# Layer 1 of a four-layer state-space kernel: which engine forms delta·u·B for half of the scan units, and where their decays lie

## The chip, the cores and the metric

The kernel runs on one core of a Trainium2 chip, in one launch, in float32. The metric is the device time of that launch in microseconds; the time of a kernel is the median of several runs.

## The reference

An image batch x (4 x 64 x 64 x 192) goes through four residual layers, each of which takes x plus a mixer of the group-normalized x. Layers 0 and 3 are two-dimensional selective scans in four directions, layer 2 is a Toeplitz mixer, and layer 1, which the change concerns, is four Mamba blocks: rows forward and backward, columns forward and backward. Each line of 64 pixels is a sequence of its own. With 384 inner channels (DI) and 16 states (DS) a block computes:

```python
def mamba_block(xs, in_w, cw, cb, xw, dtw, dtb, Alog, Dv, ow):
    ...
    uc = silu(uc + cb[None, :, None])                      # causal conv over 4 taps
    x_dbl = jnp.einsum('nld,ed->nle', uc, xw)
    dt, Bp, Cp = jnp.split(x_dbl, [DT_RANK, DT_RANK + DS], axis=-1)
    delta = jax.nn.softplus(jnp.einsum('nlr,dr->nld', dt, dtw) + dtb)
    A = -jnp.exp(Alog)
    def step(h, inp):
        d_t, b_t, c_t, u_t = inp
        dA = jnp.exp(d_t[:, :, None] * A)
        h = dA * h + (d_t * u_t)[:, :, None] * b_t[:, None, :]
        y = jnp.einsum('nds,ns->nd', h, c_t)
        return (h, y)
    ...
    y = jnp.moveaxis(ys, 0, 1) + uc * Dv
    y = y * silu(z)
    return jnp.einsum('nld,cd->nlc', y, ow)
```

For every channel and state there are thus a decay `dA`, an input `delta * u * B`, the recurrence `h`, and the product of `h` with C summed over the states.

## The kernel before, in words

Layer 1 has 4 blocks x 4 images x 8 chunks = 128 jobs of 512 pixels (8 lines of 64). A job (a "chunk") covers 384 channels in 3 tiles `t` of 128, each of two halves `c` of 64 channels. The 16 states are done in 4 pairs `p`: a unit (t, p, c) holds 64 channels x 2 halves of the states on the 128 partitions, and 2 x 512 elements along the free axis. That gives 24 units a chunk. `run_jobs` walks over all units of all chunks in one sequence; the list `TWO` gives the order of the eight units of a tile.

At position i of the sequence `run_jobs` issues, in this order:

- `feed` of unit i + 2 (`AHEAD`): it makes the two operands of the scan. The input `b` of an ordinary unit is made by TensorE in PSUM, as matmuls of `dtuT` (delta·u, transposed) with diagonal matrices `diag` that hold B, and the decays `dA` are made by ScalarE as exp(A·delta) (line 347) in one of three fixed SBUF tiles. The first element of each line has decay 0. For a *direct* unit the input is a tile `bs` that `spread` made in SBUF, and the decays go into the PSUM tile `wide` (its name in the profile is `b`), after a copy of zeros into the line starts (line 335).
- `scan` of unit i: one VectorE `tensor_tensor_scan` of 128 x 1024 (line 357) gives `h` in SBUF, then GpSimd multiplies `hc = h * cbc` (line 369), where `cbc` is C broadcast over the partitions.
- `spread` of unit i + 3 (`EARLY`), if it is direct: GpSimd multiplies `bs = dtu2 * bbc` (line 301), delta·u by B, both loaded from DRAM with broadcast.
- `collect`: TensorE sums `hc` over the states into `y` with the matrix `fold` (line 387).
- steps with a fixed position: the projections, the convolution (`input_of`, VectorE line 747), the step size and softplus, transposes, gate, output, and the loads.

Direct units before are those of pair 3, both halves: 6 of the 24, all on GpSimd. The three other pairs need `diag` tiles of B, 16 ScalarE instructions a pair and chunk (line 282). `plan` gives each load (`c`, `bc`, `both`, `dtu2`, `diag`) the position at which it is issued, after the last use of the tile whose buffer it takes. The loads go through SyncE's queue. Buffers: 3 of `h`, 5 of `hc`, 2 of `wide`/`b` in PSUM, 1 of `bs`, 4 each of `c` and `diag`, 2 of `bc`.

Layers 0 and 3 use the same functions with a state carried between chunks; their direct units are on GpSimd with decays in PSUM, and their `dtu = delta * u` (line 233) is a VectorE multiply, where layer 1's is GpSimd's. The engines' streams are filled in program order per engine, with the tile framework's ordering where nothing depends.

Of the kernel before, what the change touches and what calls it, by code (L numbers as in the profile page):

```python
# [27 lines left out]

TWO = [(0, 0), (0, 1), (3, 0), (1, 1), (1, 0), (3, 1), (2, 0), (2, 1)]
ONE = [(0, 0), (3, 0), (1, 0), (2, 0)]  # L30
LAST = 2
LEAD = 12
LEAD_DIAG = 10
D1, PD, KD = 576, 96, 6
# [2 lines left out]
class Kernel:  # L37
# [66 lines left out]
    def run_jobs(self, jobs, pools):  # L104


        G = jobs[0]["DI"] // 64
        order = []
        for t in range(-(-G // 2)):
            order += [(t, *one) for one in (TWO if 2 * t + 1 < G else ONE)]  # L110
        units = [(k, *one) for k in range(len(jobs)) for one in order]
        per = len(order)
        steps = {}
        for k, job in enumerate(jobs):
            for at, step in self.prepare(job, pools) + job["steps"]:
                steps.setdefault(k * per + at, []).append(step)
        for at, load in self.plan(jobs, order, pools):
            steps.setdefault(at, []).append(load)
        start, end = min(steps), max(len(units) + 3, max(steps) + 1)
        waiting = []  # L120
        for i in range(min(start, -EARLY), end):
            if 0 <= i + AHEAD < len(units):
                k, t, p, c = units[i + AHEAD]
                self.feed(jobs[k], t, p, c, pools)
            todo = waiting[:1]
            if 0 <= i < len(units):
                k, t, p, c = units[i]
                self.scan(jobs[k], t, p, c, pools)
            if 0 <= i + EARLY < len(units):
                k, t, p, c = units[i + EARLY]  # L130
                if c in jobs[k]["direct"].get(p, ()):
                    self.spread(jobs[k], t, p, c, pools)
            if 0 <= i < len(units):
                if (i + 1) % 2 == 0:
                    waiting += [(units[i][0], [one[1:] for one in units[i - 1 : i + 1]], n) for n in range(2)]


            if todo:
                k, two, n = waiting.pop(0)
                self.collect(jobs[k], two, n, pools)  # L140
                if n and two[1][1] == LAST:
                    jobs[k]["add"](two[0][0])
            for step in steps.get(i, []):
                step()

    def plan(self, jobs, order, pools):
# [3 lines left out]
        for k, job in enumerate(jobs):  # L150
            job["cbc"], job["bbc"], job["diag"], job["both"], job["dtu2"] = {}, {}, {}, {}, {}
            when = {name: k * len(order) + at for name, at in job["when"].items() if isinstance(at, int)}

            near = 2 if job["carry"] is not None else 5
            dtu = when["finish"] + 3 if job["carry"] is not None else when["store"] + 5
            for j, (t, p, c) in enumerate(order):
                i, g = k * len(order) + j, 2 * t + c
                direct = c in job["direct"].get(p, ())
                reads = [("c", p, i, when["project"] + 5), ("both", g, i - AHEAD, when["finish"] + near)]
                if direct:  # L160
                    reads += [("bc", p, i - EARLY, when["project"] + 5), ("dtu2", g, i - EARLY, dtu)]
                else:
                    reads.append(("diag", p, i - AHEAD, when["turn_b"] + 5))
                for name, key, at, after in reads:
                    first, _ = uses.setdefault(name, {}).get((k, key), (at, at))
                    uses[name][k, key] = first, at
                    ready[name, k] = after
        loads = []
        for name, of in uses.items():
            bufs, turn = pools["bufs"][name], sorted(of, key=of.get)  # L170
            for j, (k, key) in enumerate(turn):
                first = of[k, key][0]
                at = max(ready[name, k], first - LEAD)
                if j >= bufs:
                    at = max(at, of[turn[j - bufs]][1] + pools["behind"])
                one = lambda part=None, job=jobs[k], name=name, key=key: self.fetch(job, name, key, pools, part)
                if name == "diag":

                    at = max(ready[name, k], first - LEAD_DIAG)
                    if j >= bufs:  # L180
                        at = max(at, of[turn[j - bufs]][1] + 3)
                    loads += [(first, at + part, lambda part=part, one=one: one(part)) for part in range(NB)]
                    at += NB - 1
                else:
                    loads.append((first, at, one))
                assert at < first, (name, k, key, at, first)
# [104 lines left out]
    def spread(self, job, t, p, c, pools):  # L291

        g = 2 * t + c
        b = pools["work"].tile([128, 2 * T], F32, name="bs", bufs=1)
        if job["carry"] is None:
            by = lambda one: one.rearrange("p (h n l) -> p h n l", h=2, n=2)
            dtu = job["dtu2"][g].rearrange("p (h l) -> p h l", h=2).unsqueeze(2).broadcast_to([128, 2, 2, 256])
        else:
            by = lambda one: one.rearrange("p (n l) -> p n l", n=2)
            dtu = job["dtu2"][g].unsqueeze(1).broadcast_to([128, 2, T])  # L300
        self.nc.gpsimd.tensor_mul(by(b), dtu, by(job["bbc"][p]))  # L301
        job["bs"][t, p, c] = b

    def feed(self, job, t, p, c, pools):
# [1 line left out]
        nc = self.nc  # L306
        w, rev, g = job["w"], job["rev"], 2 * t + c
        lines = job["carry"] is None
        direct = c in job["direct"].get(p, ())
        wide = pools["b"].tile([128, 2 * T], F32, name="b")  # L310
        if direct:
            b = job["bs"].pop((t, p, c))
        else:
# [15 lines left out]
        if lines:  # L329
            if job.get("begin"):  # L330
                job.pop("begin")()
            if direct:
                dA = wide
                at = HW - 1 if rev else 0
                nc.scalar.copy(dA[:, at::HW], job["zero"])  # L335
            else:
                self.turns_dA += 1
                dA = job["dA"][self.turns_dA % len(job["dA"])]
            inner = slice(0, HW - 1) if rev else slice(1, HW)
            of = delta.rearrange("p (h a b) -> p h a b", h=2, b=HW)[:, :, :, inner]  # L340
            to = dA.rearrange("p (h n a b) -> p h n a b", h=2, n=2, b=HW)[:, :, :, :, inner]
# [27 lines left out]
        nc.gpsimd.tensor_mul(hc, h, job["cbc"][p])  # L369
        job["done"][t, p, c] = hc  # L370

    def collect(self, job, units, n, pools):

        nc = self.nc
        t, first, _ = units[0]
        last = units[1][1]
        units = sorted(units, key=lambda one: one[2])
        if first == 0 and n == 0:
            job["y"][t] = pools["y"].tile([128, T], F32, name="y")
        y = job["y"][t]  # L380
        for c, unit in enumerate(units):
# [3 lines left out]
            else:  # L385
                of = one[:, n * T : (n + 1) * T]
            nc.tensor.matmul(  # L387
                y[c * 64 : (c + 1) * 64, :], self.fold, of, start=first == 0 and n == 0, stop=last == LAST and n == 1
            )

    def neg_exp(self, A):
# [97 lines left out]
    def ss2d_scan(self, pre, u_d, y_d, P, NT, ways, A, dtb):  # L489
# [3 lines left out]
        with (  # L493
# [17 lines left out]
                for g in range(DI // 64) for p in range(PAIRS)  # L511
            }
            when = {
                3: dict(load=-33, project=-29, turn_b=-27, step_size=(-21, -19, -17), finish=-15,
                        turn=(-13, -11, -9), direct={3: (1,)}),
                2: dict(load=-25, project=-21, turn_b=-19, step_size=(-17, -16), finish=-14,
                        turn=(-9, -8), direct={3: (0, 1)}),
            }[NT]
            direct = when["direct"]

            for k, (col, rev) in sorted(enumerate(ways), key=lambda one: one[1]):
# [7 lines left out]
                for c in range(NCH - 1, -1, -1) if rev else range(NCH):  # L529
# [28 lines left out]
                    if rev:  # L558
# [1 line left out]
                            steps.append((8 * t + 2, lambda t=t, earlier=earlier: earlier(t)))  # L560
                    job.update(
                        P=P, NT=NT, DI=DI, k=k, w=w, rev=rev, carry=carry, first=first, add=add, y={}, fed={},
                        done={}, bs={}, when=when, steps=steps, direct=direct,
                    )
                    jobs.append(job)
            self.run_jobs(jobs, pools)
# [64 lines left out]
    def mamba(self, x_in):  # L631
# [6 lines left out]
        done = [self.image_tiles(f"m_out{i}_") for i in range(2)]  # L638

        both_w = [self.dram.tile([P, NT, C], F32, name=f"m_both_w{i}") for i in range(4)]  # L640
        bufs = dict(c=4, bc=2, diag=4, both=4, dtu2=2)
        with (
            tc.tile_pool(name="n", bufs=2) as pn,
            tc.tile_pool(name="n_ps", bufs=2, space=PSUM) as psum,
# [27 lines left out]
        with (  # L672
# [14 lines left out]
            pools = {"prep": prep, "work": work, "c": cp, "diag": dp, "both": both, "mm": mm, "b": bp, "y": yp,  # L687
                     "bc": bcp, "dtu2": dtu2, "bufs": bufs, "behind": 2}
            fixed = [once.tile([P, 2 * T], F32, name=f"dA{j}") for j in range(3)]
            zero = once.tile([P, 2 * ROWS], F32, name="zero")  # L690
            nc.gpsimd.memset(zero, 0.0)
            jobs = []
            for i in range(4):
                rev, w = i % 2 == 1, {}
                xs = by_row if i < 2 else by_col
                for b in range(B):
                    for c in range(NCH):
                        begin = b == 0 and c == 0
                        jobs.append(self.mamba_job(
                            pw, pin, mm, i, begin, rev, w, xs[b], done[i // 2][b], both_w[i], c, fixed, zero  # L700
                        ))
            self.run_jobs(jobs, pools)
        return list(zip(*done))

    def mamba_job(self, pw, pin, mm, i, begin, rev, w, x, done, both_w, c, fixed, zero):

        nc, ins = self.nc, self.i
        P, NT = 128, 3
# [72 lines left out]
                nc.scalar.copy(o, ps)  # L781
            nc.sync.dma_start(done[:, m, s], o)

        when = dict(project=-24, turn_b=-22, step_size=(-20, -18, -17), finish=-15, turn=(-10, -7, -3), store=-11)
        each = lambda f, ats: [(at, lambda t=t: f(t)) for t, at in enumerate(ats)]
        steps = [(-50, weights)] if begin else []
        steps += [(-48, load)] + each(input_of, (-45, -32, -29)) + each(gate, (-6, -4, -2)) + each(out, (32, 35))
        if rev:
            steps += each(earlier, (26, 29))
        job.update(  # L790
            P=P, NT=NT, DI=DI, w=w, rev=rev, carry=None, first=True, dA=fixed, y={}, fed={}, done={}, bs={},
            add=gated, when=when, steps=steps, begin=start_lines if begin else None, direct={3: (0, 1)},
            zero=zero,
        )
        return job

# [309 lines left out]
```

## Time and profile before

| what | value |
|---|---|
| median of 3 runs | 31,847.99 us (31,831.84 to 31,864.97) |
| the profiled execution's own time | 31,794.9 us |
| its span | 31,793.1 us, mean granted TensorE clock 0.948 |
| layer 1's scans, first to last | 11,042.1 to 22,312.9 us |
| busy share of the whole span | PE 89%, DVE 71%, ACT 73%, POOL 71% |
| busy share, 12,000 to 22,000 us | PE 95%, DVE 72%, ACT 82%, POOL 88% |

PE is TensorE, DVE is VectorE, ACT is ScalarE, POOL is GpSimd, and SP is SyncE. A line of the profile names the source line, the engine, the operation, the tiles as output<-inputs, shapes, and the count, then the busy time in us and the mean duration of one in ns, and after the second bar the time the engine stood idle before these instructions with what ended it. Matmuls overlap, so a count times a mean can exceed the busy time; a float32 matmul appears as two instructions. In the timeline a line has the start in us and the duration in us first; neighbours of one kind are merged (x2, x3).

### The profile page before, as it was taken

Reading aid. Unit: us, or ns where it says so; the run is one execution under the profiler, and the core shown is the slowest. Engines: PE = TensorE matmul, PEld = TensorE weight load, DVE = VectorE, ACT = ScalarE, POOL = GpSimd, SP = SyncE. Lnnn points to the kernel's source line nnn. Section 1 sums busy time; section 2 is a strip of 40 time slices with the busy share of each in tenths; the row PEclk is TensorE's granted clock in tenths of the full one; section 3 lists DMA queues with packets and bytes.
Section 4 is the critical chain, followed back from the end, with each engine's and each line's share of the span. In section 5 each row is a group of like instructions: output and inputs, shape, how many; then the busy total and the mean of one; then the engine's idle time right before and its main releaser. Section 6 shows DMA issues by size and latency. Waiting matters only on the chain. (4 is left out here: it accounts for less than half of the span.)

```text
span 31793.1 us, 449637 instructions
## 1 busy us (share of the span) xinstructions
PE 28311.3 (89%) x162840; PEld 13772.2 (43%) x162840; DVE 22474.8 (71%) x16587; ACT 23362.1 (73%) x50239; POOL 22678.0 (71%) x9755
## 2 busy tenths in 40 slices
PE   8997998999899699999999999999588988888888
PEld 4453554454445344444444444444355343434344
DVE  7887887788788677777777777777433267676767
ACT  7885885887688488888888888888133287878788
POOL 6884885888488488888888888888000086767777
PEclk9998999999999899999999999999788999999999
DMA  3333333333333423233333333333533444444444
GB/s 101 100 97 110 99 97 107 103 98 98 109 100 97 135 93 93 93 97 98 98 98 96 95 95 95 98 98 99 132 72 72 109 129 120 128 124 125 124 124 124
DMA packets 1565670, 3326.87 MB, mean 105 GB/s; under 512 B 343781, under 2 KB 356438, under 8 KB 1546934
## 3 DMA queue, kind: packets, MB, share of 16 engines
q1 hardware_dynamic: 1403702, 3021.19, 34.7%
q10 hardware_dynamic: 159744, 276.91, 2.6%
q8 instruction: 1289, 21.12, 0.3%
q14 instruction: 935, 7.66, 0.1%
HBM read 2137.94 MB, written 656.08 MB: 88 GB/s over the span
## 5 line engine op out<-in xcount | busy, mean ns | idle before, releaser
L369 POOL TENSOR_TENSOR hc<-h,c 128x1024 f32<-128x1024 f32 x7680 | 18189.2, 2384 | 3115.9 <-DVE h L364 1317.7
L324 PE MATMUL b<-diag,dtuT 128*64 128x256 f32 x98304 | 12805.9, 391 | 800.1 <-DVE h L364 679.9
L324 PEld LDWEIGHTS b<-diag,dtuT 128*64 128x64 f32 x98304 | 7507.3, 140 | 6835.9 <-issue 3091.1
L387 PE MATMUL y<-hc,fold 128*64 128x512 f32 x30720 | 8995.0, 598 | 587.4 <-POOL hc L369 572.6
L364 DVE TENSOR_TENSOR_SCAN h<-dA,carry,b 128x512 f32<-128x512 f32 x6720 | 8195.0, 1264 | 1805.9 <-PE b L324 1134.3
L347 ACT ACTIVATE dA<-both,A 128x512 f32<-128x512 f32 (+1 forms) x12288 | 8279.8, 711 | 203.0 <-DVE h L357 182.0
L357 DVE TENSOR_TENSOR_SCAN h<-dA,b 128x1024 f32<-128x1024 f32 x2304 | 5251.7, 2284 | 2047.7 <-PE b L324 883.2
L282 ACT ACTIVATE diag<-ident,bt 128x128 f32<-128x128 f32 x20480 | 6527.3, 391 | 124.5 <-ACT b L347 86.1
L301 POOL TENSOR_TENSOR bs<-dtu,bc 128x1024 f32<-128x1024 f32 x1536 | 3638.4, 2369 | 1479.7 <-DMA c<-bc_dram 1087.9
L387 PEld LDWEIGHTS y<-hc,fold 128*64 128x64 f32 x30720 | 2497.6, 138 | 2981.7 <-POOL hc L369 1262.0
L441 POOL MEMSET pad<- 128x13068 f32 (+1 forms) x8 | 73.4, 9177 | 3977.5 <-DMA inw<-in_L_in_w 3004.7
L347 ACT ACTIVATE b<-both,A 128x504 f32<-128x504 f32 (+1 forms) x3072 | 2078.1, 676 | 412.7 <-DVE h L364 379.8
L357 DVE TENSOR_TENSOR_SCAN h<-b,bs 128x1024 f32<-128x1024 f32 x768 | 1754.1, 2284 | 659.6 <-ACT b L347 391.2
L367 ACT COPY carry<-h 128x2 f32<-128x2 f32 x4608 | 851.4, 185 | 1367.1 <-DVE h L364 1165.5
L364 DVE TENSOR_TENSOR_SCAN h<-b,carry,bs 128x512 f32<-128x512 f32 x1344 | 1638.0, 1259 | 105.7 <-POOL hc L369 95.3
L364 DVE TENSOR_TENSOR_SCAN h<-dA,b 128x512 f32<-128x512 f32 x960 | 1112.9, 1205 | 436.2 <-ACT dA L347 175.8
L347 ACT ACT_TABLE_LOAD x1018 | 1306.1, 1283 | 15.0 <-ACT b L335 0.3
L730 PE MATMUL in_ps<-xn,in_w 96*128 96x512 f32 x1536 | 933.4, 738 | 329.4 <-DMA xn<-m_row 177.8
L747 DVE SCALAR_TENSOR_TENSOR u<-in_ps,conv_w,u 128x504 f32<-128x504 f32 (+2 forms) x1152 | 835.7, 725 | 460.3 <-ACT u L742 438.6
L233 DVE TENSOR_TENSOR dtu<-delta,u 128x1536 f32<-128x1536 f32 (+1 forms) x256 | 611.4, 2388 | 758.2 <-ACT delta L232 602.9
L242 PEld LDWEIGHTS dtu_ps<-ident,dtu 128*128 128x128 f32 (+1 forms) x4096 | 422.1, 142 | 875.7 <-issue 569.3
L730 PE MATMUL z_ps<-xn,in_w 96*128 96x512 f32 x1536 | 761.7, 618 | 0.0
(155 smaller groups left out, 22077.8 us busy)
## 6 DMA issues: line engine op xcount, KB each, us to landing
c<-bc_dram SPq DMA_DIRECT2D x3072, 256.0 KB
both<-delta SPq DMA_DIRECT2D x2048, 128.0 KB
bc<-bc_dram SPq DMA_DIRECT2D x768, 256.0 KB
both<-delta_dram SPq DMA_DIRECT2D x768, 256.0 KB
dtu<-dtu_dram SPq DMA_DIRECT2D x768, 256.0 KB
dtu<-dtu SPq DMA_DIRECT2D x1280, 128.0 KB
L_y<-out ACTq DMA_DIRECT2D x512, 256.0 KB
u<-L_u SPq DMA_DIRECT2D x160, 768.0 KB
```

The source lines that it names most:

```text
L233: (nc.gpsimd if job["carry"] is None else nc.vector).tensor_mul(job["dtu"], delta, job["u"])
L282: nc.scalar.activation(to, self.ident, AF.Copy, scale=of)
L301: self.nc.gpsimd.tensor_mul(by(b), dtu, by(job["bbc"][p]))
L324: nc.tensor.matmul(to, job["dtuT"][:, k, g * 64 : (g + 1) * 64], job["diag"][p][:, k, 2 * q : 2 * q + 2, :], start=True, stop=True,)
L347: nc.scalar.activation(to[n], of, AF.Exp, scale=w["A"][:, g, 2 * p + n : 2 * p + n + 1])
L357: nc.vector.tensor_tensor_scan(h[:, way], dA[:, way], b[:, way], 0.0, ALU.mult, ALU.add)
L364: nc.vector.tensor_tensor_scan(hn[:, n, way], dA[:, n, way], by_n[:, n, way], start, ALU.mult, ALU.add)
L367: nc.scalar.copy(carry[g, p], hn[:, :, 0 if rev else T - 1])
L369: nc.gpsimd.tensor_mul(hc, h, job["cbc"][p])
L387: nc.tensor.matmul(y[c * 64 : (c + 1) * 64, :], self.fold, of, start=first == 0 and n == 0, stop=last == LAST and n == 1)
L730: nc.tensor.matmul(ps, w["in_w"][:, k, to + t * P : to + (t + 1) * P], job["xn"][:, k, :], start=k == 0, stop=k == KC - 1,)
L747: nc.vector.scalar_tensor_tensor(u[:, :, to], ps[:, :, of], tap(3 - j), u[:, :, to], ALU.mult, ALU.add)
```

## The change

In layer 1 direct units become those of pairs 1 and 3: 12 of the 24 units of a chunk. For (1, 0), (1, 1) and (3, 0) `spread` runs on VectorE, for (3, 1) on GpSimd: with three tiles, nine and three a chunk. `direct` is now a dictionary from (pair, half) to engine. A direct unit of layer 1 takes its decays from the same three fixed SBUF tiles `dA` as the others and no PSUM tile, and the copy of zeros is gone. The order of units in a tile becomes `LINES`, in which ordinary and direct units alternate; `collect` learns from `run_jobs` which pair of units is the first and last of a tile (`ends`). There are two `bs` buffers in layer 1, three of `bc` and three of `diag`; a `diag` buffer is refilled 2 positions after its last use in layer 1 in place of 3; some steps move by one to six positions. Layers 0 and 3 keep their units, engines and order.

```diff
+LINES = [(0, 0), (3, 1), (2, 0), (1, 1), (0, 1), (3, 0), (2, 1), (1, 0)]
...
-                if c in jobs[k]["direct"].get(p, ()):
+                if (p, c) in jobs[k]["direct"]:
                     self.spread(jobs[k], t, p, c, pools)
...
-                        at = max(at, of[turn[j - bufs]][1] + 3)
+                        at = max(at, of[turn[j - bufs]][1] + pools["behind"])
...
     def spread(self, job, t, p, c, pools):
-        b = pools["work"].tile([128, 2 * T], F32, name="bs", bufs=1)
+        b = pools["work"].tile([128, 2 * T], F32, name="bs", bufs=2 if job["carry"] is None else 1)
...
-        self.nc.gpsimd.tensor_mul(by(b), dtu, by(job["bbc"][p]))
+        job["direct"][p, c].tensor_mul(by(b), dtu, by(job["bbc"][p]))
...
     def feed(self, job, t, p, c, pools):
-        direct = c in job["direct"].get(p, ())
-        wide = pools["b"].tile([128, 2 * T], F32, name="b")
+        direct = (p, c) in job["direct"]
+        wide = None if direct and lines else pools["b"].tile([128, 2 * T], F32, name="b")
...
-            if direct:
-                dA = wide
-                at = HW - 1 if rev else 0
-                nc.scalar.copy(dA[:, at::HW], job["zero"])
-            else:
-                self.turns_dA += 1
-                dA = job["dA"][self.turns_dA % len(job["dA"])]
+            self.turns_dA += 1
+            dA = job["dA"][self.turns_dA % len(job["dA"])]
...
     def mamba(self, x_in):
-        bufs = dict(c=4, bc=2, diag=4, both=4, dtu2=2)
+        bufs = dict(c=4, bc=3, diag=3, both=4, dtu2=2)
...
-        when = dict(project=-24, turn_b=-22, step_size=(-20, -18, -17), finish=-15, turn=(-10, -7, -3), store=-11)
+        when = dict(project=-23, turn_b=-21, step_size=(-19, -18, -17), finish=-15, turn=(-9, -7, 3), store=-11)
...
-        steps += [(-48, load)] + each(input_of, (-45, -32, -29)) + each(gate, (-6, -4, -2)) + each(out, (32, 35))
+        steps += [(-48, load)] + each(input_of, (-45, -33, -29)) + each(gate, (-5, -3, -1)) + each(out, (33, 35))
...
-            add=gated, when=when, steps=steps, begin=start_lines if begin else None, direct={3: (0, 1)},
-            zero=zero,
+            add=gated, when=when, steps=steps, begin=start_lines if begin else None, turns=LINES,
+            direct={(1, 0): nc.vector, (1, 1): nc.vector, (3, 0): nc.vector, (3, 1): nc.gpsimd},
```

More of the change, by code (lines that the diff above doesn't have):

```diff
@@ L30 @@
 ONE = [(0, 0), (3, 0), (1, 0), (2, 0)]
-LAST = 2
+LINES = [(0, 0), (3, 1), (2, 0), (1, 1), (0, 1), (3, 0), (2, 1), (1, 0)]
 LEAD = 12
@@ L109, in run_jobs @@
         for t in range(-(-G // 2)):
-            order += [(t, *one) for one in (TWO if 2 * t + 1 < G else ONE)]
+            order += [(t, *one) for one in (jobs[0]["turns"] if 2 * t + 1 < G else ONE)]
         units = [(k, *one) for k in range(len(jobs)) for one in order]
@@ L134, in run_jobs @@
                 if (i + 1) % 2 == 0:
-                    waiting += [(units[i][0], [one[1:] for one in units[i - 1 : i + 1]], n) for n in range(2)]
+                    tile = units[i][:2]
+                    ends = [j < 0 or j >= len(units) or units[j][:2] != tile for j in (i - 2, i + 1)]
+                    waiting += [(units[i][0], [one[1:] for one in units[i - 1 : i + 1]], n, ends) for n in range(2)]
             if todo:
-                k, two, n = waiting.pop(0)
-                self.collect(jobs[k], two, n, pools)
-                if n and two[1][1] == LAST:
+                k, two, n, ends = waiting.pop(0)
+                self.collect(jobs[k], two, n, ends, pools)
+                if n and ends[1]:
                     jobs[k]["add"](two[0][0])
@@ L308, in feed @@
         lines = job["carry"] is None
-        direct = c in job["direct"].get(p, ())
-        wide = pools["b"].tile([128, 2 * T], F32, name="b")
+        direct = (p, c) in job["direct"]
+        wide = None if direct and lines else pools["b"].tile([128, 2 * T], F32, name="b")
         if direct:
@@ L370, in scan, with collect @@
         job["done"][t, p, c] = hc
-    def collect(self, job, units, n, pools):
+    def collect(self, job, units, n, ends, pools):
         nc = self.nc
-        t, first, _ = units[0]
-        last = units[1][1]
+        t, (first, last) = units[0][0], ends
         units = sorted(units, key=lambda one: one[2])
-        if first == 0 and n == 0:
+        if first and n == 0:
             job["y"][t] = pools["y"].tile([128, T], F32, name="y")
@@ L387, in collect @@
             nc.tensor.matmul(
-                y[c * 64 : (c + 1) * 64, :], self.fold, of, start=first == 0 and n == 0, stop=last == LAST and n == 1
+                y[c * 64 : (c + 1) * 64, :], self.fold, of, start=first and n == 0, stop=last and n == 1
             )
@@ L514, in ss2d_scan @@
                 3: dict(load=-33, project=-29, turn_b=-27, step_size=(-21, -19, -17), finish=-15,
-                        turn=(-13, -11, -9), direct={3: (1,)}),
+                        turn=(-13, -11, -9), direct={(3, 1): nc.gpsimd}),
                 2: dict(load=-25, project=-21, turn_b=-19, step_size=(-17, -16), finish=-14,
-                        turn=(-9, -8), direct={3: (0, 1)}),
+                        turn=(-9, -8), direct={(3, 0): nc.gpsimd, (3, 1): nc.gpsimd}),
             }[NT]
@@ L562, in ss2d_scan @@
                         P=P, NT=NT, DI=DI, k=k, w=w, rev=rev, carry=carry, first=first, add=add, y={}, fed={},
-                        done={}, bs={}, when=when, steps=steps, direct=direct,
+                        done={}, bs={}, when=when, steps=steps, direct=direct, turns=TWO,
                     )
@@ L689, in mamba @@
             fixed = [once.tile([P, 2 * T], F32, name=f"dA{j}") for j in range(3)]
-            zero = once.tile([P, 2 * ROWS], F32, name="zero")
-            nc.gpsimd.memset(zero, 0.0)
             jobs = []
@@ L699, in mamba @@
                         jobs.append(self.mamba_job(
-                            pw, pin, mm, i, begin, rev, w, xs[b], done[i // 2][b], both_w[i], c, fixed, zero
+                            pw, pin, mm, i, begin, rev, w, xs[b], done[i // 2][b], both_w[i], c, fixed
                         ))
@@ L703, in mamba, with mamba_job @@
         return list(zip(*done))
-    def mamba_job(self, pw, pin, mm, i, begin, rev, w, x, done, both_w, c, fixed, zero):
+    def mamba_job(self, pw, pin, mm, i, begin, rev, w, x, done, both_w, c, fixed):
         nc, ins = self.nc, self.i
```

## The prediction

> **What bounds layer 1 now.** I read first the busy time of each engine in a steady stretch of layer 1 (12,000 to 22,000 us), then the groups of instructions there, then single stretches of the timeline in which VectorE and GpSimd meet.
>
> The stretch, busy us by engine (PE, PEld, DVE, ACT, POOL), clock and DMA:
>
> ```profile
> 12000.00:22000.00 10000.00, 9466.04 (x50885) 4135.91 (x50882) 7181.93 (x4210) 8205.20 (x15114) 8768.51 (x3872) 0.97 0.31 97
> ```
>
> Its groups (busy us, mean ns | idle before):
>
> ```profile
> L369 POOL TENSOR_TENSOR hc<-h,c 128x1024 f32<-128x1024 f32 x2727 | 6411.3, 2368 | 1231.5 <-DVE h L357 1113.7 <-PE b L324 89.7 <-DMA c<-bc_dram 17.0
> L357 DVE TENSOR_TENSOR_SCAN h<-dA,b 128x1024 f32<-128x1024 f32 x2045 | 4661.7, 2284 | 1787.9 <-PE b L324 755.6 <-ACT dA L347 704.8 <-POOL hc L369 203.3
> L324 PE MATMUL b<-diag,dtuT 128*64 128x256 f32 x32704 | 4094.3, 392 | 102.2 <-DVE h L357 102.2
> ...
> L282 ACT ACTIVATE diag<-ident,bt 128x128 f32<-128x128 f32 x5460 | 1746.4, 390 | 91.0 <-ACT b L347 78.5 <-DMA dtu<-dtu_dram 12.5
> L301 POOL TENSOR_TENSOR bs<-dtu,bc 128x1024 f32<-128x1024 f32 x682 | 1617.7, 2372 | 0.0
> L357 DVE TENSOR_TENSOR_SCAN h<-b,bs 128x1024 f32<-128x1024 f32 x681 | 1555.3, 2284 | 578.9 <-ACT b L347 348.7 <-POOL bs L301 174.8 <-POOL dtu L233 48.9
> ```
>
> Six bs a chunk, so 682 of them are 113.67 chunks: 87.97 us a chunk, 3.67 us for each of its 24 units. Per chunk PE is busy 83.3 us (95%), POOL 77.1, ACT 72.2, DVE 63.2. PE is the fullest, and scans wait for b from it. The reader is to see one thing more: a scan takes the same 2284 ns in both forms, and hc keeps 2368 ns beside them. In both forms one of the scan's two inputs is in PSUM: b where dA is in SBUF, and the decays (tile "b") where bs is in SBUF.
>
> What a DVE instruction with two SBUF inputs does beside GpSimd is shown only in the other layers, by `dtu = delta * u` (L233). Alone, a multiply of that size takes 1758 ns; L233 takes 3030 (groups of the whole run):
>
> ```profile
> L233 DVE TENSOR_TENSOR dtu<-delta,u 128x1536 f32<-128x1536 f32 x128 | 387.9, 3030 | 442.3 <-ACT delta L232 287.0 <-DMA c<-bc_dram 155.3
> ...
> L619 DVE TENSOR_TENSOR yc<-yc,z 128x1536 f32<-128x1536 f32 x32 | 56.3, 1758 | 39.5 <-ACT yc L616 38.7
> ```
>
> The timeline (start us, duration us) in layer 0, and in layer 3 where GpSimd came second:
>
> ```profile
> 2278.42 2.37 POOL L369 TENSOR_TENSOR hc<-h,c 128x1024 f32<-128x1024 f32 x1 [1.07 <-PE b L324]
> 2279.33 3.07 DVE L233 TENSOR_TENSOR dtu<-delta,u 128x1536 f32<-128x1536 f32 x1 [1.08 <-ACT delta L232]
> ```
>
> ```profile
> 26120.84 5.66 POOL L369 TENSOR_TENSOR hc<-h,c 128x1024 f32<-128x1024 f32 x2
> ...
> 26122.05 2.23 DVE L233 TENSOR_TENSOR dtu<-delta,u 96x1024 f32<-96x1024 f32 x1
> ```
>
> Layer 0: hc ends at 2280.79, DVE at 2282.40, 1.61 us later: 1536 elements at the rate of the lone multiply, so DVE did nothing while hc ran. Layer 3: the second hc of the two ends at 26126.50, 2.22 us after DVE's end at 26124.28: it did nothing while DVE ran. DVE there ends 1.08 us after the hc it waited for (single records). The two engines exclude each other.
>
> **What the Trainium skill says.** Its page "SBUF — State Buffer", section "Who interferes with whom", says that a DVE instruction with two SBUF inputs contends with a GpSimd instruction that reads SBUF, that the one which comes second is blocked until the first is over, and that one SBUF input outside the two-port modes does not contend. The lines above agree for multiplies (both directions) and for scans with one SBUF input. No run here shows a scan with two. "VectorE: DVE Perf Modes", section "The perf-mode tier table", has float32 tensor_tensor at 1x only: agreed, L619 is 1.14 ns an element.
>
> **The change part by part, per chunk of layer 1.** The order of instructions after the change gives the counts; the other layers keep theirs.
>
> - PE: six more direct units, so 18 b units become 12. b is 4094.3/113.67 = 36.0 us, 2.0 a unit: −12.0, PE 71.
> - ACT: diagonals for two pairs in place of three: −16 x 0.32 (1746.4/5460) = −5.1; six zero copies of 172 ns: −1.0; two table loads of 1283 ns fewer: −2.6; the 12 decays move to SBUF (707 ns for 671): about 0. ACT 63.5.
> - POOL: three bs of 2.37 fewer: −7.1, POOL 70.0.
> - DVE: nine multiplies of 128x1024. Nearest row: the lone 96x1024 multiplies, 1.20 us. +10.8, DVE 74.0.
> - SP: two bc loads of 256 KB more, 0.46 us each to issue, DMA at 31%: hidden. The new turn order leaves three units between the last use of a c tile and the next chunk's first, where the tightest pair had four: at the new pace (below) 13.4 us instead of 14.7, and hc waited only 17.0 us for c in the whole stretch: 0, at worst 1 to 3 us for each of four c loads. PSUM and dA buffers: the b tiles now serve half the units, so PE's waits for a scan shrink; three diag buffers in place of four delay ACT, which has slack.
>
> By these sums alone no engine would exceed 74 us. But the 12 direct scans now read dA **and** bs from SBUF, and the nine DVE multiplies read two SBUF tensors. All 21 must exclude every GpSimd instruction, and all of GpSimd's work here reads SBUF. The added wait is on both engines: behind a blocked multiply stands the next scan on DVE, behind a blocked hc the next hc and the bs, and y on PE waits for hc.
>
> The excluded time per chunk, by durations after a handover: a direct scan 2.28 − 0.13 = 2.15 (0.13 is what the multiply's lone 1.20–1.22 exceeds its 1.08 by; applied to the scan, an estimate), a DVE multiply 1.08, hc 2.22 after DVE and 2.32 after another POOL instruction (pitch of successive hc in the stretch). DVE's order is direct scan, multiply, other scan; two units thus cost 2.15 + 1.08 + 2.22 + 2.32 = 7.77 us, while the other scan (2.28) runs beside hc. Twelve such: 93.2. Three of the multiplies are POOL's: +3 x (2.32 − 1.08) = 3.7. z in gated 3 x 1.25 = 3.8; dtu 3.4. Sum **104.2 us**, above every engine's own load, and above 87.97. DVE's convolution and gate (9.4 us, one input in PSUM) hide under hc. Idle of the shared interface: none at best, and 5.3% if it idles like PE now; I take the middle, 2.65%: 107.0 us a chunk, 4.46 a unit.
>
> 107.0 − 87.97 = 19.1 us; x128 chunks = 2,440 us. The profiled execution took 31,794.9 (span 31,793.1), so 34,235; the median of the runs is 53 above that execution: **34,290 us**. Unknown costs of this case: idle 0 gives +2,080 (33,920), idle 8% with late c loads +3,300 (35,150).
>
> **The rivals.**
>
> 1. Faster: the scan, at 2.2 ns an element half the multiply's pace, does not take the shared interface; only the nine multiplies do. Against it: the skill's rule names any two-input instruction. For it: no scan with two SBUF inputs has been seen. Then POOL decides: 70.0 + 9 x (1.08 + 2.22 − 2.32 = 0.98) = 78.8, and with PE's 5.3% idle 83.2 us: −4.8 x 128 = −610, **31,240 us**. It tips to slower if exclusion from scans exceeds 4.8/12 = 0.4 us each.
> 2. Half exclusion: the scan holds the interface for half of its time: 104.2 − 12 x 1.08 = 91.2, /0.9735 = 93.7: +730, **32,580 us**. Against it: in the multiplies the exclusion was whole.
> 3. Exclusion plus lost cover: the scheduled order leaves hc with nothing ready while other scans run, a tenth of the time: 104.2/0.89 = 117: +3,720, **35,570 us**. For it: hc waits 1113.7 us for scans already. Against it: h and hc have 3 and 5 buffers, so GpSimd can lag and keep work ready.
> 4. No effect: exclusion from scans happens to cancel PE's relief; a narrow point between 1 and 2.
>
> **How the numbers follow.** Full exclusion 0.79, rival 1 0.09, rival 2 0.07, rival 3 0.04, rival 4 0.01. A measurement of this kernel tells about 0.2% from no change. Faster 0.09, within 0.01, slower 0.90. The range leaves out rival 1 and most of 2 and 3: 32,900 to 35,300.
>
> **What would show it.** Right: in layer 1 the busy shares of PE and ACT fall to about 66% and 59% (71 and 63.5 of 107 us), while those of DVE and POOL stay high, because a blocked instruction's record is stretched by its wait (L233 above); direct scans with dA and bs have a mean well above 2284 ns, or hc well above 2368, and the multiplies well above 1200; where the two engines meet, hc ends about 2.2 us after a direct scan's end; diag falls to 32 a chunk. Wrong: direct scans and hc overlap with both at their old durations, and the chunk is about 83 us.

## The result, and the profile after

The changed kernel took 35,047.84 us (median of 4 runs, 35,042.67 to 35,054.36), the kernel before 31,839.92 us in the same comparison: a ratio of 1.1009, 95% interval 1.099 to 1.1028. It is 3,208 us slower. The forecast was 34,290 us, range 32,900 to 35,300; its mechanism is borne out by what follows, one term of its sum is not. The loss is in layer 1: its scans now run from 11,051 to 25,556 us of the profiled execution (own time 35,042.67 us), 14,504 us in place of 11,271.

The busy time of each engine in a steady stretch of layer 1 of the changed kernel, columns as before:

```profile
13000.00:24000.00 11000.00, 8356.57 (x34060) 3161.98 (x34058) 9230.93 (x4454) 6783.02 (x10943) 9708.15 (x3010) 0.89 0.26 79
```

The groups of that stretch (busy us, mean ns | idle before):

```profile
L366 POOL TENSOR_TENSOR hc<-h,c 128x1024 f32<-128x1024 f32 x2323 | 7564.1, 3276 | 918.6 <-DVE h L354 885.7 <-DMA c<-bc_dram 7.0 <-PE y L383 1.7
L354 DVE TENSOR_TENSOR_SCAN h<-dA,bs 128x1024 f32<-128x1024 f32 x1161 | 3627.7, 3125 | 703.1 <-ACT dA L344 358.2 <-POOL hc L366 329.7 <-POOL dA L754 10.1
...
L326 PE MATMUL b<-diag,dtuT 128*64 128x256 f32 x18578 | 2830.6, 400 | 154.4 <-DVE h L354 154.2
L354 DVE TENSOR_TENSOR_SCAN h<-dA,b 128x1024 f32<-128x1024 f32 x1161 | 2637.3, 2272 | 530.0 <-PE b L326 510.7 <-POOL dA L754 19.3
L303 DVE TENSOR_TENSOR bs<-dtu,bc 128x1024 f32<-128x1024 f32 x871 | 2302.6, 2644 | 21.6
...
L303 POOL TENSOR_TENSOR bs<-dtu,bc 128x1024 f32<-128x1024 f32 x290 | 1065.8, 3675 | 0.0
L284 ACT ACTIVATE diag<-ident,bt 128x128 f32<-128x128 f32 x3104 | 980.8, 388 | 0.0
```

2323 hc are 96.8 chunks: **113.7 us a chunk**, where before it was 88.0. Diagonals are 32 a chunk, as the diff says. The scans with one SBUF input (dA and b) kept their time, 2272 ns. Everything that reads two SBUF tensors grew: the direct scans to 3125 ns, the VectorE multiplies to 2644 (1.2 alone), hc from 2368 to 3276, GpSimd's bs from 2372 to 3675. These records hold waiting time, as the timeline of the changed kernel shows (start us, duration us; each line a neighbour of the one before on the other engine):

```profile
18029.37 4.64 POOL L366 TENSOR_TENSOR hc<-h,c 128x1024 f32<-128x1024 f32 x2
18031.75 4.42 DVE L354 TENSOR_TENSOR_SCAN h<-dA,bs 128x1024 f32<-128x1024 f32 x1 [3.40 <-POOL hc L366]
18033.97 4.34 POOL L303 TENSOR_TENSOR bs<-dtu,bc 128x1024 f32<-128x1024 f32 x1
18036.20 3.19 DVE L303 TENSOR_TENSOR bs<-dtu,bc 128x1024 f32<-128x1024 f32 x1
```

The two hc end at 18034.01. The direct scan, on record since 18031.75, ends 2.16 us later, at 18036.17. The bs of GpSimd, on record since 18033.97, ends 2.14 us after the scan, and the VectorE multiply 1.08 us after that. The four run one after the other though their records overlap by half: **the scan with two SBUF inputs excludes GpSimd just as the multiply does.**

To measure this over the whole stretch I put GpSimd's instructions and VectorE's two-input ones in the order of their ends, and count for each the time from the later of its own start and the end before it. Where an instruction was already waiting at that end, the means are 2.155 us for a direct scan (the prediction's 2.15), 1.083 for a VectorE multiply (1.08), 2.18 for hc behind VectorE (2.22) and 2.31 behind GpSimd (2.32). Per chunk all these records cover 103.3 us, where the prediction's sum was 104.2. For 10.4 us none of them is on record; that I call the idle time of the interface, which stands for whatever it is that the two engines cannot use at once. The same count for the kernel before gives 77.2 covered and 10.8 idle.

### The profile page after: what moved, and what is told of

Same layout as the page of the kernel before. It is cut to its first block, busy times and chain, and to the rows that moved or that the text cites. A ratio compares the mean times of both kernels' runs of the same rounds, so it can differ in the third digit from the quotient of the medians.

```text
span 35040.9 us, 424437 instructions
## 1 busy us (share of the span) xinstructions
PE 28695.3 (82%) x150552; PEld 13290.8 (38%) x150552; DVE 26610.9 (76%) x17739; ACT 23085.3 (66%) x47679; POOL 25626.4 (73%) x9370
## 5 line engine op out<-in xcount | busy, mean ns | idle before, releaser
L366 POOL TENSOR_TENSOR hc<-h,c 128x1024 f32<-128x1024 f32 x7680 | 20946.8, 2744 | 2927.7 <-DVE h L361 1381.5
L383 PE MATMUL y<-hc,fold 128*64 128x512 f32 x30720 | 10270.2, 654 | 3548.5 <-POOL hc L366 3548.5
L326 PE MATMUL b<-diag,dtuT 128*64 128x256 f32 x86016 | 11929.6, 394 | 883.4 <-DVE h L361 680.4
L344 ACT ACTIVATE dA<-both,A 128x512 f32<-128x512 f32 (+1 forms) x13824 | 9175.7, 710 | 2411.3 <-DVE h L354 2313.9
L284 ACT ACTIVATE diag<-ident,bt 128x128 f32<-128x128 f32 x18432 | 5855.7, 390 | 26.4 <-issue 0.9
L354 DVE TENSOR_TENSOR_SCAN h<-dA,bs 128x1024 f32<-128x1024 f32 x1536 | 4815.9, 3135 | 922.9 <-ACT dA L344 469.2
L354 DVE TENSOR_TENSOR_SCAN h<-dA,b 128x1024 f32<-128x1024 f32 x1536 | 3489.0, 2271 | 679.1 <-PE b L326 658.0
L303 DVE TENSOR_TENSOR bs<-dtu,bc 128x1024 f32<-128x1024 f32 x1152 | 3040.9, 2640 | 37.6 <-DMA dtu<-dtu_dram 9.1
L361 DVE TENSOR_TENSOR_SCAN h<-b,carry,bs 128x512 f32<-128x512 f32 x1344 | 1638.3, 1260 | 104.2 <-POOL hc L366 93.6
L344 ACT ACT_TABLE_LOAD x1146 | 1470.3, 1283 | 20.2 <-DMA both<-delta_dram 3.0
L344 ACT ACTIVATE b<-both,A 128x512 f32<-128x512 f32 x1536 | 1047.1, 682 | 409.5 <-DVE h L361 378.9
L759 POOL TENSOR_TENSOR z<-z,u 128x512 f32<-128x512 f32 x384 | 752.6, 1960 | 487.3 <-DVE u L758 477.3
L744 ACT ACT_TABLE_LOAD x381 | 488.8, 1283 | 787.9 <-DVE u L741 785.6
```

What stands on the lines that cost most here:

```text
L284: nc.scalar.activation(to, self.ident, AF.Copy, scale=of)
L303: job["direct"][p, c].tensor_mul(by(b), dtu, by(job["bbc"][p]))
L326: nc.tensor.matmul(to, job["dtuT"][:, k, g * 64 : (g + 1) * 64], job["diag"][p][:, k, 2 * q : 2 * q + 2, :], start=True, stop=True,)
L344: nc.scalar.activation(to[n], of, AF.Exp, scale=w["A"][:, g, 2 * p + n : 2 * p + n + 1])
L354: nc.vector.tensor_tensor_scan(h[:, way], dA[:, way], b[:, way], 0.0, ALU.mult, ALU.add)
L361: nc.vector.tensor_tensor_scan(hn[:, n, way], dA[:, n, way], by_n[:, n, way], start, ALU.mult, ALU.add)
```

## The experiments

All are timed against the kernel before on the same chip, whose median was 31,832 to 31,846 us in these comparisons; the changed kernel's own time is the one above. The idle and the covered time are counted as above, between 13,000 and 21,500 us.

**One part alone: decays in SBUF.** The kernel before, whose six direct units stay on GpSimd, with their decays in the fixed SBUF tiles:

```diff
-        wide = pools["b"].tile([128, 2 * T], F32, name="b")
+        wide = None if direct and lines else pools["b"].tile([128, 2 * T], F32, name="b")
...
-            if direct:
-                dA = wide
-                at = HW - 1 if rev else 0
-                nc.scalar.copy(dA[:, at::HW], job["zero"])
-            else:
-                self.turns_dA += 1
-                dA = job["dA"][self.turns_dA % len(job["dA"])]
+            self.turns_dA += 1
+            dA = job["dA"][self.turns_dA % len(job["dA"])]
```

> The kernel before with one part of the change alone: its six direct units a chunk (all on GpSimd) take their decays from the fixed SBUF tiles, without zero copies. Theory (exclusion): the six direct scans have a mean well above 2284 ns where they come second; the excluded time is 77.2 + 6 x 2.15 - 6 x 0.14 = 89.3 us a chunk, with 2 to 11 us of idle 91.5 to 100 us, so 32,300 to 33,400 us. Rival (a scan does not need the shared interface, the multiplies on VectorE made the loss): no slower than before, 31,500 to 31,900 us, since PSUM is relieved.

32,538.16 us, ratio 1.022 (1.0205 to 1.0235). The groups of this kernel in the stretch:

```profile
L352 DVE TENSOR_TENSOR_SCAN h<-dA,b 128x1024 f32<-128x1024 f32 x1631 | 3715.3, 2283 | 1676.6 <-ACT dA L342 671.9 <-POOL hc L364 443.6 <-PE b L324 264.0
L352 DVE TENSOR_TENSOR_SCAN h<-dA,bs 128x1024 f32<-128x1024 f32 x544 | 1831.5, 3367 | 71.1 <-POOL bs L301 59.2 <-ACT dA L342 0.5
```

```profile
L364 POOL TENSOR_TENSOR hc<-h,c 128x1024 f32<-128x1024 f32 x2175 | 5985.2, 2776 | 454.5 <-DVE h L352 450.4 <-issue 2.0 <-PE in_ps L725 1.5
```

No multiply has moved, yet scans with two SBUF inputs take 3367 ns and those with one 2283, and hc is 408 ns longer than before. Covered time 89.0 us a chunk (expected 89.3), idle 4.8, chunk 93.8. The exclusion by scans is shown by itself: moving one operand from PSUM to SBUF costs about 700 us with six such scans a chunk. The edit also makes the three fixed decay tiles serve all 24 units in place of 18; but the covered time alone, 89.0 us, is already more than the 88.0 us of a whole chunk before, and VectorE's waits for decays hold 1.0 us of the idle here against 1.4 before, so late decays do not make the loss.

**Another part alone: multiplies on VectorE.** The kernel before with its six multiplies on the other engine:

```diff
-        self.nc.gpsimd.tensor_mul(by(b), dtu, by(job["bbc"][p]))
+        (self.nc.vector if job["carry"] is None else self.nc.gpsimd).tensor_mul(by(b), dtu, by(job["bbc"][p]))
```

> The kernel before with another part alone: its six multiplies for bs a chunk on VectorE in place of GpSimd, decays in PSUM. Theory (exclusion whole but short for multiplies): excluded time 77.2 - 6 x 2.32 + 6 x 1.08 = 69.8 us, VectorE 63.2 + 6 x 1.2 and up to 1.2 us of waiting for each, 78 us at most, PE unchanged at 83 of 88 us: within 1% of before, 31,550 to 32,150 us. Rival (VectorE multiplies stall the scans in front of GpSimd so that most of the loss comes from them): above 32,500 us.

31,868.73 us, ratio 1.0012 (1.0003 to 1.0021). The VectorE multiplies of this kernel:

```profile
L301 DVE TENSOR_TENSOR bs<-dtu,bc 128x1024 f32<-128x1024 f32 x576 | 1172.4, 2035 | 11.2
```

Each waits 0.8 us on average (2035 − 1.2 us alone), and still the covered time falls to 69.8 us a chunk, as expected, and the time stays; the idle is 18.7 us, and TensorE, 92% busy, is the fullest engine here too. The multiplies exclude GpSimd too, but briefly, and they free more of GpSimd (2.32 us each) than they take (1.08). By themselves they are not the loss.

**The change with its decays back in PSUM.** `dA = wide` with its PSUM tile and the zero copy as in the lines removed above, all else as changed.

> The changed kernel with the decays of its 12 direct units a chunk back in PSUM (and the zero copies back); the nine VectorE and three GpSimd multiplies, the unit order and the step positions stay as changed. Theory (scans with two SBUF inputs exclude GpSimd): every scan is back at about 2284 ns and hc beside a scan at 2368; the excluded time falls from the 103.3 us a chunk measured after the change by 12 x 2.16 to about 77 us; with 2 to 10 us of idle a chunk that is 79 to 87.5 us, so 30,750 to 31,850 us in all. Rival (the VectorE multiplies, the unit order or the smaller diag and larger bc pools cost the time): it stays above 33,500 us.

33,048.72 us, ratio 1.038 (1.0363 to 1.0398): 2,000 us faster than the changed kernel, but above what the theory allowed. The groups of this kernel in the stretch:

```profile
L373 POOL TENSOR_TENSOR hc<-h,c 128x1024 f32<-128x1024 f32 x2084 | 5546.1, 2679 | 1203.8 <-DVE h L361 1086.9 <-DMA c<-bc_dram 92.3 <-PE y L390 1.1
...
L361 DVE TENSOR_TENSOR_SCAN h<-b,bs 128x1024 f32<-128x1024 f32 x1041 | 2372.6, 2279 | 462.3 <-ACT b L351 462.0 <-issue 0.3
L361 DVE TENSOR_TENSOR_SCAN h<-dA,b 128x1024 f32<-128x1024 f32 x1042 | 2369.9, 2274 | 495.1 <-PE b L328 375.4 <-ACT dA L351 82.9 <-POOL hc L373 23.2
```

Both kinds of scan are back at 2.28 us, and the covered time falls from 103.3 to 79.4 us. But the idle rises from 10.4 to 18.5: the interface no longer decides, and scans wait for decays and for b in PSUM, and the gate for y. So about 2,000 of the 3,208 us go with the exclusion by scans. The order, the pools and steps of the change, or twelve direct units on two PSUM tiles, carry a cost of their own of about 1,200 us when that exclusion is gone; which of them it is, no run separates.

**Where the idle of the changed kernel comes from.** The idle was the term furthest from the forecast, so five runs went to it. The largest waits of VectorE between 13,000 and 24,000 us (96.8 chunks; total us, times, longest us):

```profile
DVE h L354 <- PE b L326: 510.7, 97, 5.6
DVE u L758 <- PE y L383: 507.4, 97, 6.0
DVE h L354 <- ACT dA L344: 358.2, 94, 4.2
DVE h L354 <- POOL hc L366: 329.7, 97, 3.4
```

A wait of VectorE leaves the interface idle only if GpSimd has nothing to do meanwhile. Laid over the idle time (13,000 to 21,500 us), the wait for b holds 3.1 us of it a chunk and the gate's wait for y 3.0; the waits for decays and for hc hold none, since GpSimd works through them. Another 3.5 us pass while an ordinary scan runs and GpSimd has no new h. The place of the gate in the timeline:

```profile
18074.64 3.32 POOL L366 TENSOR_TENSOR hc<-h,c 128x1024 f32<-128x1024 f32 x1 [2.29 <-DVE h L354]
18078.01 3.59 PE L383 MATMUL y<-hc,fold 128*64 128x512 f32 x8 [2.94 <-POOL hc L366]
...
18081.68 0.75 DVE L758 SCALAR_TENSOR_TENSOR u<-u,D,y 128x512 f32<-128x512 f32 x1 [5.93 <-PE y L383]
...
18082.44 2.28 DVE L354 TENSOR_TENSOR_SCAN h<-dA,b 128x1024 f32<-128x1024 f32 x1
18082.51 1.27 POOL L759 TENSOR_TENSOR z<-z,u 128x512 f32<-128x512 f32 x1 [4.55 <-DVE u L758]
```

hc ends at 18077.96, y needs it, the gate (L758) needs y, and the next scan stands behind the gate in VectorE's queue; GpSimd, with no new h, waits 4.55 us. The place of b comes next:

```profile
18092.37 1.98 PE L383 MATMUL y<-hc,fold 128*64 128x512 f32 x4 [1.73 <-POOL hc L366]
...
18094.13 1.07 PE L326 MATMUL b<-diag,dtuT 128*64 128x256 f32 x4
...
18095.38 2.29 DVE L354 TENSOR_TENSOR_SCAN h<-dA,b 128x1024 f32<-128x1024 f32 x1 [5.26 <-PE b L326]
```

In TensorE's queue y, which waits for hc, stands in front of b.

First, the convolution's nine VectorE instructions a chunk left out, taps and all:

```diff
-            for j in range(1, 4):
+            for j in range(4, 4):
                 to, of = slice(j, HW), slice(0, HW - j)
```

> The changed kernel without the nine VectorE instructions a chunk of layer 1's convolution (the taps other than the last are left out of the computation, 6.5 us of VectorE a chunk). In the changed kernel the shared interface stands idle 10.4 us a chunk, 5.3 of them in one place: ScalarE waits for the convolution on VectorE, the decays behind it come late, and the direct scan with them. Theory: that idle goes, and the chunk falls by 4 to 6 us to 108 to 110 us, 34,300 to 34,550 us in all. Rival (the convolution was hidden under hc, as predicted, and the idle has another cause): within 0.5% of the changed kernel, 34,900 to 35,200 us.

34,967.39 us, ratio 1.0983 (1.0966 to 1.0999); idle 10.3, as in the changed kernel; the 80 us are little more than the noise of the two ratios. The theory missed because it had laid 5.3 us of the idle to late decays; in the trace of the changed kernel they stand at the scan that waits for b, 3.1 us of waiting and 2.2 us in which that scan itself runs. VectorE's wait for decays did fall, from 277.9 to 88.3 us in the stretch, but no idle was behind it. The wait for b stayed, behind the same y:

```profile
17034.81 7.47 POOL L366 TENSOR_TENSOR hc<-h,c 128x1024 f32<-128x1024 f32 x2 [0.98 <-DVE h L354]
...
17042.34 1.97 PE L383 MATMUL y<-hc,fold 128*64 128x512 f32 x4 [1.73 <-POOL hc L366]
17044.10 1.07 PE L326 MATMUL b<-diag,dtuT 128*64 128x256 f32 x4
...
17045.34 2.29 DVE L354 TENSOR_TENSOR_SCAN h<-dA,b 128x1024 f32<-128x1024 f32 x1 [5.26 <-PE b L326]
```

The second hc ends at 17042.28, y follows at once, then b, then the scan. Second, therefore, `collect` (y, and with it the gate) one unit later in layer 1:

```diff
...
-            todo = waiting[:1]
+            todo = waiting[(1 if jobs[0]["carry"] is None and i < len(units) else 0) :][:1]
```

> The changed kernel with the summing matmuls (y from hc, in collect) and the gate that follows them one unit later in layer 1. In the changed kernel the shared interface stands idle 10.4 us a chunk. Theory: the idle comes from in-order queues behind hc: y waits for a late hc at the head of TensorE's queue with the b matmuls of coming scans behind it, and the gate on VectorE waits for y with the next scan behind it. Then the idle falls to 3 to 6 us a chunk, 34,050 to 34,500 us in all. Rival (idle from late decays or from too few tiles in flight): within 0.5% of the changed kernel, or slower because the five hc buffers are held longer, 34,900 us or more.

34,691.31 us, ratio 1.0898 (1.0882 to 1.0914): 357 us faster than the changed kernel, idle 7.5 us. The direction is the theory's, the size about half of the middle of what it expected: the idle in the waits for b and y falls from 6.1 to 0.9 us, but that beside ordinary scans rises from 3.5 to 5.1, and 1.0 us in waits for decays is new. Third, both edits:

> The changed kernel with collect one unit later in layer 1 and also without the nine VectorE instructions a chunk of the convolution (the taps other than the last are left out of the computation). Idle of the shared interface so far, us a chunk: changed kernel 10.4, without convolution 10.3, collect later 7.5, where the largest idle left (3.0) stands at a direct scan whose decays come late from ScalarE, which waited for the convolution. Theory: the two causes mask each other, so with both gone the idle falls to 2 to 5 us and the chunk to 105 to 108 us, 33,950 to 34,350 us in all. Rival (what is left has a third cause): idle stays at 7 us or more, 34,600 us or more.

34,504.8 us, ratio 1.0838 (1.0822 to 1.0854), idle 6.3. Between theory and rival: the convolution is worth 187 us here and about 80 alone, so its cost is in part masked, but 6 us stay. Some of VectorE's waits left in this kernel:

```profile
DVE u L758 <- PE y L383: 536.7, 110, 7.0
DVE h L354 <- ACT dA L344: 221.2, 77, 5.6
DVE h L354 <- PE b L326: 140.7, 78, 1.8
```

The idle of these kernels, us a chunk from 13,000 to 21,500 us, by what VectorE does meanwhile (small remainders left out; in the kernel before it is GpSimd's idle time; 10.3 is the 10.4 above, in the shorter stretch):

| kernel | scan waits for b | gate waits for y | scan waits for decays | an ordinary scan runs | all |
|---|---|---|---|---|---|
| before | 0.2 | 0.0 | 1.4 | 8.9 | 10.8 |
| changed | 3.1 | 3.0 | 0.0 | 3.5 | 10.3 |
| no convolution | 3.0 | 3.4 | 0.0 | 3.2 | 10.3 |
| later `collect` | 0.8 | 0.0 | 1.0 | 5.1 | 7.5 |
| both | 0.7 | 2.2 | 0.0 | 2.7 | 6.3 |

In the last kernel the gate's wait for y is again the largest of the waits. The 3.0 us that the expectation of this run puts down to late decays stand, in the trace of the later `collect`, at the scan that waits for b and follows it.

Fourth, the gate alone one unit later in the code, behind the next scan:

> The changed kernel with the gate alone (the VectorE instruction that reads y, and GpSimd's product behind it) behind the next scan in layer 1; the summing matmuls stay where they are. In the changed kernel 4.5 us of the idle a chunk stand at this place: the next scan is queued behind the gate, the gate waits for y, y for hc. Theory: that idle goes and part of it comes back elsewhere, as with collect one unit later (idle 7.5, 34,691 us): 34,450 to 34,800 us. Rival (the b matmuls behind y in TensorE's queue are the tighter wait, and the gate is not decisive): 34,900 to 35,150 us.

35,132.32 us, ratio 1.1036 (1.1018 to 1.1055), idle 10.7. This run tells nothing about the gate that waits: of the three gates a chunk that one (5.2 us of waiting on average) stands in front of the same scan as in the changed kernel, and the edit did not move it. What moved, in 61 of the 128 chunks, is another gate, which never waited.

Fifth, the later `collect` (by two units, with six hc buffers and two fixed decay tiles) in the kernel with decays in PSUM:

> Decays of the direct units in PSUM as in the run of that name, and collect two units later in layer 1, with six hc buffers and two fixed decay tiles in place of five and three. There the excluded time was 79.5 us a chunk and the idle 18.5. Theory (in-order queues behind hc): the idle falls to 6 to 12 us, the chunk to 85.5 to 91.5 us, 31,450 to 32,250 us in all. Rival (VectorE and ScalarE wait for PSUM tiles, two for all units): no change, 32,900 to 33,200 us.

32,900.2 us, ratio 1.0336 (1.0318 to 1.0353), idle 17.7 after 18.5: the lower edge of the rival's figure. The gate's wait for y fell from 818.0 to 433.0 us in the stretch, the time by only 148 us. But ScalarE now waits 339.1 us for scans before it can write the fixed decay tiles, a wait that was absent with three of them, so the run does not settle whether the queue behind hc holds this kernel up. Whether the rest is the two PSUM tiles, the unit order or the step positions, no run separates.

**The kernel before with the later `collect`.**

> The kernel before with collect one unit later in layer 1 and nothing else. Theory (TensorE is the bound at 95% there and little of its time is waiting for hc): within 0.5% of before, 31,700 to 32,000 us. Rival (y at the head of TensorE's queue costs there too): 31,000 to 31,600 us.

32,145.33 us, ratio 1.0098 (1.0083 to 1.0113): slower than either expectation. Its waits (13,000 to 21,500 us) show what is late instead:

```profile
POOL hc L369 <- DMA c<-bc_dram: 608.1, 85, 10.4
```

This wait was 17.0 us in the steady stretch before. Once in nearly every chunk (93.5 in its stretch) hc waits some 7 us for a c tile. ScalarE's wait for z, 642.0 us, is new as well; why both come, no run shows. The edit is no free gain. None of the versions beats the kernel before; the nearest, the multiplies on VectorE, equals it.

## Why the prediction was right or wrong, point by point

- **The exclusion and its size: right.** The sum of 104.2 us a chunk was measured at 103.3, each of its four durations within 0.04 us of its term (the terms as printed add up to 104.1). That a scan with two SBUF inputs excludes GpSimd was argued from multiplies and from the rule of the Trainium skill ("SBUF — State Buffer", section "Who interferes with whom"); the decays-in-SBUF run agrees with it, with only the place of the decays changed: 3367 ns for such a scan against 2283. Rivals 1 and 2 (no exclusion by scans, half of it) fall.
- **The idle: mis-sized.** The term is "5.3% if it idles like PE now; I take the middle, 2.65%", a middle with no reading of the trace behind it. It measured 9.1% (10.4 of 113.7 us). In us a chunk: 113.7 − 107.0 = 6.7, of which the idle is +7.6 and the covered time −0.9; x128 that is 860 us, about the 758 us between forecast and median. The measured time is in fact nearer to rival 3 (522 us off), which was given 0.04, and whose idle of a tenth was nearly right (it divides by 0.89; a tenth would give about 35,410 us). Its mechanism, hc with nothing ready while ordinary scans run, is 3.5 of the 10.4 us. GpSimd before already stood idle 10.8 us a chunk, and the profile said that it waits for h; I put that down to PE being the bound and let it go with PE's load. That the two sizes agree is chance: before, 8.9 us of it passed beside ordinary scans; after, 6.1 us are the waits for b and y.
- **"h and hc have 3 and 5 buffers, so GpSimd can lag and keep work ready": wrong in part.** Buffers let it lag; the queues do not. y on TensorE and the gate on VectorE wait for hc in program order, with the next b and the next scan behind them. Moving both later gave back 357 us; what would remove the rest of the idle is not settled.
- **"Convolution and gate hide under hc": right for the convolution** in this kernel (about 80 us when left out), wrong for the gate's place: it is not its 0.7 us but the wait for y in front of the next scan.
- **Shares of PE and ACT:** expected 66% and 59%, measured 76% and 62%. b took 29.2 us of TensorE's busy time a chunk where 12 units at 2.0 us made 24, and y 36.5 where it took 26.5 before, with as many matmuls: the busy time of a group before was not a price for it after. On ScalarE "two table loads of 1283 ns fewer" was wrong: there are 14 a chunk after 12, four more than the sum had, 5.1 us. As neither engine was the bound, the forecast did not suffer.
- **The late c loads, priced at nothing to 3 us each: right at nothing.** hc waited 7.0 us for c in the whole stretch, less than before.
- **The forecast of POOL and DVE shares** (high, because records stretch): right, 88% and 84%.

## What to carry to other kernels

Before moving an operand of a VectorE instruction from PSUM to SBUF, count its SBUF inputs: in this case a second one made float32 scans and multiplies exclude GpSimd's multiplies for their whole length (2.155 and 1.083 us behind a handover), and the two engines' times had then to be added, not laid side by side. Price such a change by summing the excluded instructions of both engines, with durations taken behind a handover; here that gave the load within 1%. Then look for the chain that makes the shared resource idle (who waits in order behind the last result); here it idled 9.1% of the time, where the busiest engine before had idled 5.3%. And before blaming a wait, look whether the shared resource is idle during it: VectorE's 3.7 us of waiting for decays a chunk cost nothing.

## What the runs showed of the hardware that was not expected

TensorE's granted clock in layer 1 fell from 0.97 to 0.89 as TensorE became less busy (95% to 76%); without the convolution it was 0.87 at 77% busy. The stretches of all eleven kernels agree: 0.96 to 0.98 in the four where TensorE was busy 91% or more, 0.87 to 0.93 in the seven where it was busy 84% or less. What is cause and what is effect, no run here shows, and in the changed kernel TensorE was not the bound.

A handover from VectorE to GpSimd adds no time that the records show: hc takes 2.18 us behind a VectorE instruction that it waited for, 2.31 behind another GpSimd instruction, and its unhindered record before is 2.37. Why the first is the shortest, no run shows.
